# The last token pair of a fused attention and feed-forward kernel: base product undivided, maxima by halves, another order of steps

## The chip, the core and the metric

The kernel runs on one core of a Trainium2 chip. PE is the matrix engine, PEld its weight loads, DVE, ACT and POOL are the vector, scalar and general engines, and SP issues most of the transfers. The metric is the device time of one execution in microseconds; less is better.

## What is computed

The input `x` has 64 batches of 64 tokens of 1024 values, float32. Two blocks are added to it in turn:

```python
x = x + attention(conditioned(x, itok_B_0_15, W_cond))
x = x + ffn(cond2(x, itok_B_0_7))

def cond2(x, ids):                     # W: (1024, 1024), 8 experts of rank 16
    base = x @ W.T
    logits = x @ Wr.T + 5.0 * one_hot(ids)
    gates = softmax over the two largest logits, 0 elsewhere
    return base + 2.0 * einsum(x @ A.T, gates, B)

def ffn(z):                            # z rounded to bfloat16
    qg, sg = quant(z, inv_gate)        # per token: scale = max|z*inv| / 127, round, clip
    qu, su = quant(z, inv_up)
    inter = clip(silu(qg @ Wg.T * sg * s_wgate) * (qu @ Wu.T * su * s_wup), -10, 10)
    qi, si = quant(bf16(inter), inv_inter)
    return qi @ Wd.T * si * s_wdown
```

The change lies in the base product, the quantizations and what follows them, for the last 256 tokens.

## The kernel before

The attention with its output projection comes first; its result and its transpose go to device memory. From 1763.4 us on, `second_stage` works through 16 pairs (`p`), each of two tiles (`t`) of 128 tokens. Within it every instruction is issued in the order in which the helpers are called: the schedule is written by hand, three pairs deep. While pair `p` is at its base product, pair `q = p - 1` is at gate and up, and `r = p - 2` at its end. The last turn (`p, q, r` = 15, 14, 13) is a list of its own after the loop, and drains all three.

The helpers, for a pair `p` and a tile `t`:

- `router` (L1300) and `route` (DVE, small instructions L1316 to L1347) give the gates; `gates_transposed` (L1360) turns them on PE, ACT copies them to `gT`.
- `token_sums` (L1041 to L1044) makes four sums of token blocks on DVE, and `base(p, i)` (L1031) the seven products of a Strassen-Winograd scheme: the 256 x 1024 by 1024 x 1024 product is divided in 2 x 2 x 2 blocks, and seven block products of four float32 matmuls (128 x 128 by 128 x 512) take the place of eight. The weights lie in quarters `A11`, `A12`, `A22` and in combined quarters `S1` to `S4`, in tiles `wtA..` and `wtS..`. `lora` (L1365) adds the expert part by one matmul per output half. `after(p, i)` (L1389 to L1403) combines the products on DVE, two of them by an ACT copy, and writes `z` in bfloat16.
- `quant_a(p, t, nm)` for `nm` of g, u and i (gate, up, inter): multiply (L1413), maximum (L1417), scale (L1419), reciprocal (L1421) on DVE, then two roundings on ACT (L1422, L1424). `quant_b` clips on DVE (L1432) and transposes the result, by a transfer from SP (L1435), or with `by_pe=True` by matmuls (L1439) and an ACT copy (L1440).
- `gate_or_up` (L1449) is eight bfloat16 matmuls, `scaled` (L1454) multiplies by the scales on DVE and for g takes a sigmoid on ACT (L1460), `glu` (L1466 to L1469) multiplies, clips and rounds on DVE.
- `down` (L1478) is two halves of four bfloat16 matmuls; `result` multiplies by the scales (L1487) and then either hands the tile to a transfer from POOL that adds it in device memory (L1495), or adds `x` on the engine named (L1491) and stores it from SP (L1492).

Two pools of four PSUM banks, `ps_g` and `ps_h`, hold the products. A tile of a pool waits until the buffer it takes has been read by its last user. `q` and `y` in the pool `p2` have two buffers each, so have the small tiles of `sm`.

Of the kernel before, what the change touches and what calls it, by code (L numbers as in the profile page):

```python
# [11 lines left out]
F32 = mybir.dt.float32  # L12
BF16 = mybir.dt.bfloat16
# [1174 lines left out]
def second_stage(tc, a, out_t, xT_d, ident, ps_g, KC, NT, H, C, half, comb, op):  # L1188
# [12 lines left out]
    with ExitStack() as ctx:  # L1201
# [162 lines left out]
        def lora(p, ps, t, wts):  # L1364
            nc.tensor.matmul(ps, st[p]["gT"][:, t, :], wts, start=False, stop=True, skip_group_check=True)  # L1365
# [14 lines left out]

        def lora_5(p):
            lora(p, st[p]["ps", 5], 1, bm[:, hs[1]])
# [22 lines left out]
        def quant_a(p, t, nm, between=None):  # L1405
# [12 lines left out]
            sc = s["sc", nm, t] = sm.tile([P, 1], F32, tag="sc" + nm, name=f"sc_{nm}_{p}_{t}")  # L1418
# [53 lines left out]
        def down(p, t):  # L1472
            s = st[p]
            qT = s.pop(("qT", "i", t))
            for n in range(2):
                ps = s["pd", t, n] = ps_h.tile([P, HH], F32, tag="h", name=f"pd_{p}_{t}_{n}")
                for k in range(IC):
                    nc.tensor.matmul(  # L1478
                        ps, qT[:, k, :], wt_b["wd"][:, k, hs[n]], start=(k == 0), stop=(k == IC - 1)
                    )  # L1480

        def result(p, t, adds=None):
            s = st[p]
            y = p2.tile([P, H], F32, tag="y", name=f"y_{p}_{t}")
            si = s.pop(("sc", "i", t))
            for n in range(2):
                nc.vector.scalar_tensor_tensor(  # L1487
                    y[:, hs[n]], s.pop(("pd", t, n)), si, sd_w[:, hs[n]], ALU.mult, ALU.mult
                )
                if adds:  # L1490
                    adds.tensor_add(y[:, hs[n]], y[:, hs[n]], s["x", t][:, hs[n]])  # L1491
                    nc.sync.dma_start(out_t[2 * p + t, :, hs[n]], y[:, hs[n]])  # L1492
            if not adds:

                nc.gpsimd.dma_start(out_t[2 * p + t], y, accum_op=ALU.add)  # L1495

        def do(when, f, *args):
            if when:
                f(*args)
# [3 lines left out]
        for p in range(NPAIR - 1):  # L1503
# [18 lines left out]
            base(p, 7)  # L1522
            do(last, down, r, 1)
# [42 lines left out]
        token_sums(p)  # L1566
        quant_a(r, 1, "i")
        base(p, 1)
        after(p, 1)
# [3 lines left out]
        base(p, 6)  # L1573
        base(p, 7)
        gates_transposed(p)
        after(p, 6)
        quant_a(q, 0, "u")
        base(p, 2)
        after(p, 2)
        after(p, 7)  # L1580
        quant_a(q, 1, "g", (q, 0, "u"))
        down(r, 1)
        result(r, 1)
        quant_a(q, 1, "u", (q, 1, "g"))
        gate_or_up(q, 0, "g")
        scaled(q, 0, "g")
        base(p, 4)
        after(p, 4)
        gate_or_up(q, 0, "u")
        quant_a(p, 0, "g", (q, 1, "u"))  # L1590
        scaled(q, 0, "u")
        base(p, 5)
        lora_5(p)
        after(p, 5)
        quant_a(p, 0, "u", (p, 0, "g"))
        glu(q, 0)
        gate_or_up(q, 1, "g")
        quant_b(p, 0, "u")
        base(p, 3)
        scaled(q, 1, "g")  # L1600
        after(p, 3)
        gate_or_up(q, 1, "u")
        quant_a(p, 1, "g")
        gate_or_up(p, 0, "g")
        scaled(q, 1, "u")
        quant_a(p, 1, "u", (p, 1, "g"))
        gate_or_up(p, 0, "u")
        quant_a(q, 0, "i")
        glu(q, 1)
        quant_b(p, 1, "u", True)  # L1610
        gate_or_up(p, 1, "g")
        quant_a(q, 1, "i", (q, 0, "i"))
        gate_or_up(p, 1, "u")
        down(q, 0)
        scaled(p, 0, "g")
        scaled(p, 0, "u")
        quant_b(q, 1, "i")
        glu(p, 0)
        scaled(p, 1, "g")
        scaled(p, 1, "u")  # L1620
        result(q, 0)
        quant_a(p, 0, "i")
        down(q, 1)
        glu(p, 1)
        quant_b(p, 0, "i", True)
        result(q, 1, nc.gpsimd)
        quant_a(p, 1, "i")
        down(p, 0)
        result(p, 0, nc.gpsimd)
        quant_b(p, 1, "i", True)  # L1630
# [56 lines left out]
```

## Time and profile before

| | us |
|---|---|
| median of 3 runs | 2462.17 |
| lowest, highest | 2460.88, 2463.17 |
| the profiled execution, its time | 2461.01 |
| the profiled execution, its span | 2459.1 |
| start of the router of pair 15 on PE | 2376.60 |
| last base product of pair 15 starts on PE | 2412.34 |
| reciprocal of i, pair 15 tile 1, on DVE | 2445.20 |
| last down product starts on PE | 2448.87 |
| last addition on DVE starts | 2453.29 |

Times inside the execution count from the start of its span. A row of the order of instructions (the timeline) has: start, duration, engine, line, operation, output<-inputs, shapes, count, and in brackets how long the engine was idle before it and what ended that. Rows of one kind that follow each other are merged: "x8" is eight matmuls. The end of a PE row is modelled and overlaps the start of the next row by about 0.16 us. A row of busy time by stretches has: the stretch, its length, busy time of PE, PEld, DVE, ACT and POOL with the number of instructions, the clock granted to PE as a share of full speed, the share of the transfer engines, GB/s.

### The profile page before, as it was taken

The numbers are of one execution on the slowest core, as the hardware profiler recorded it, in microseconds if no ns is written. First come the engines' busy times: TensorE is split into PE (matmuls) and PEld (weight loads), VectorE is DVE, ScalarE is ACT, GpSimd is POOL, SyncE is SP. The second block draws the span as 40 slices with busy tenths as digits, with TensorE's granted clock in tenths as the row PEclk, the third lists the DMA queues.
The fourth block names the chain that finished last, engine by engine and source line by source line (L and its number), as shares of the span: only waits on it lengthen the run. The fifth ranks groups of instructions, "written<-read, shape, count | busy, mean of one in ns | idle before, by whom it ended". The sixth has DMA issues, their size and how long they took to land.

```text
span 2459.1 us, 34200 instructions
## 1 busy us (share of the span) xinstructions
PE 2423.2 (99%) x13194; PEld 1699.6 (69%) x13232; DVE 1533.1 (62%) x2957; ACT 952.8 (39%) x1303; POOL 363.4 (15%) x451
## 2 busy tenths in 40 slices
PE   8999999999999999999999999999999999999996
PEld 7888888888888888888888544444454545454452
DVE  4685585775664755745646623333367777778787
ACT  1353353342443533534424544344323333333333
POOL 5110001011122221210000233333200000000001
PEclk9999999999999999999999999999999999999998
DMA  8895767676677767775547588876744344434343
GB/s 280 284 264 152 219 200 238 188 208 210 201 198 250 206 194 246 207 208 175 177 137 234 170 258 255 263 243 215 242 126 83 84 79 88 80 81 87 70 95 72
DMA packets 417980, 446.76 MB, mean 182 GB/s; under 512 B 299665, under 2 KB 353938, under 8 KB 404114
## 3 DMA queue, kind: packets, MB, share of 16 engines
q1 hardware_dynamic: 387298, 377.90, 52.9%
q0 software_dynamic: 12080, 49.82, 7.7%
q10 hardware_dynamic: 18432, 16.79, 2.0%
q8 instruction: 106, 1.74, 0.3%
q14 instruction: 64, 0.52, 0.1%
HBM read 272.97 MB, written 100.66 MB: 152 GB/s over the span
## 4 chain that ended last, share of the span: by engine, by line
PE 94%; DVE 2%; ACT 2%; DMA 1%; issue 0%; ACTq 0%; SPq 0%; DVEq 0%
PE psva L462 5%; PE pska L435 5%; PE psvd L462 5%; PE psqa L435 5%; PE psvc L462 4%; PE pbc L1031 4%; PE pba L1031 4%; PE psqc L435 4%; PE pskc L435 4%; PE psqd L435 4%; PE pskd L435 4%; PE pbd L1031 4%; PE poa L1031 4%; PE pod L1031 4%; PE poc L1031 4%; PE s L498 3%
## 5 line engine op out<-in xcount | busy, mean ns | idle before, releaser
L540 ACT COPY pT<-phT 128x1024 int16<-128x1024 int16 x128 | 167.2, 1342 | 84.8 <-DMA phT<-ph 84.6
L514 ACT ACTIVATE prob<-prob 128x512 f32<-128x512 f32 x128 | 80.6, 630 | 259.4 <-DVE prob L511 232.1
L421 DVE SCALAR_TENSOR_TENSOR kbd<-pskd,bqkv,psku 32x256 f32<-32x256 f32 x256 | 123.1, 481 | 31.6 <-PE pskd L435 27.8
L528 ACT COPY ph<-prob 128x1024 int16<-128x1024 int16 x128 | 130.8, 1047 | 24.3 <-DVE prob L522 23.7
L1152 POOL TENSOR_TENSOR xo<-xo,ob 128x1024 f32<-128x1024 f32 x32 | 84.1, 2648 | 351.7 <-DVE To L1042 305.5
L561 ACT ACTIVATE co<-c,bqkv 128x256 f32<-128x256 f32 x128 | 60.1, 469 | 179.6 <-PE c L550 152.1
L435 PE MATMUL psqa<-yB,wq 128*128 128x256 f32 x512 | 123.6, 384 | 0.5 <-ACT psqp L406 0.5
L435 PE MATMUL pska<-yB,wk 128*128 128x256 f32 x512 | 122.6, 382 | 0.0
L1495 POOL DMA_DIRECT2D out_dram<-y x29 | 25.2, 869 | 652.3 <-DVE y L1487 652.3
L1126 ACT COPY xh<-xo 128x1024 int16<-128x1024 int16 x64 | 64.1, 1040 | 142.4 <-DVE xo L1171 142.4
L462 PE MATMUL psva<-wv,yB 128*128 128x256 f32 x512 | 117.0, 382 | 0.4
L1031 PE MATMUL poa<-woA,cx 128*128 128x512 f32 x256 | 115.4, 593 | 0.0
L1031 PE MATMUL pba<-wtA,x1T 128*128 128x512 f32 x256 | 115.1, 592 | 0.0
L1137 ACT COPY xTo<-xhT 128x1024 int16<-128x1024 int16 x64 | 84.7, 1339 | 58.4 <-DMA xhT<-xh 52.1
L435 PEld LDWEIGHTS pska<-yB,wk 128*128 128x128 f32 x512 | 96.0, 190 | 15.0 <-issue 2.6
L435 PEld LDWEIGHTS psqa<-yB,wq 128*128 128x128 f32 x512 | 95.2, 190 | 16.0 <-issue 2.8
L462 PEld LDWEIGHTS psva<-wv,yB 128*128 128x128 f32 x512 | 96.1, 190 | 14.1 <-ACT yB L363 1.0
L510 DVE TENSOR_REDUCE mx<-s 128x8 f32<-128x512 f32 x128 | 87.7, 685 | 10.7 <-PE s L498 9.3
L511 DVE TENSOR_TENSOR prob<-s,mx 128x512 f32<-128x512 f32 x128 | 88.5, 691 | 9.3 <-DVE mx L510 0.5
L522 DVE TENSOR_TENSOR prob<-prob,den 128x512 f32<-128x512 f32 x128 | 88.5, 692 | 4.4
L520 DVE TENSOR_REDUCE den<-prob 128x8 f32<-128x512 f32 x128 | 86.7, 678 | 7.2 <-ACT prob L514 6.3
L1031 PEld LDWEIGHTS poa<-woA,cx 128*128 128x128 f32 x256 | 48.4, 190 | 60.1 <-issue 59.9
(243 smaller groups left out, 5135.5 us busy)
## 6 DMA issues: line engine op xcount, KB each, us to landing
wv<-v_d SPq DMA_DIRECT2D x98, 512.0 KB, 3.9
wq<-q_d SPq DMA_DIRECT2D x28, 1792.0 KB, 7.7
wk<-k_d SPq DMA_DIRECT2D x28, 1792.0 KB, 8.1
x<-in_x_dram SPq DMA_DIRECT2D x32, 512.0 KB, 9.1
ctx_d<-co ACTq DMA_DIRECT2D x128, 128.0 KB, 4.2
cx<-ctx_d SPq DMA_DIRECT2D x16, 1024.0 KB, 6.9
xo<-in_x_dram SPq DMA_DIRECT2D x32, 512.0 KB, 5.7
xT_d<-xTo SPq DMA_DIRECT2D x64, 256.0 KB, 3.2
```

Of the source, the lines that this page charges most:

```text
L421: nc.vector.scalar_tensor_tensor(dst, ps, bias, u, ALU.add, ALU.add)
L435: nc.tensor.matmul(ps[:, 0:HB], A[:, SLOT[A_OF[i]], k, :], B[B_OF[i]][:, k, :], start=first and k == 0, stop=k == KQ - 1, skip_group_check ...
L462: nc.tensor.matmul(ps[:, j * VC:(j + 1) * VC], B[B_OF[i]][:, k, j * P:(j + 1) * P], A[:, k, :], start=first and j == 0 and k == 0, stop=k ...
L510: nc.vector.tensor_reduce(mx_v, ps, AX.X, ALU.max)
L511: nc.vector.tensor_tensor(p.rearrange("p (a e) k -> p a e k", a=2), ps, mx_v.unsqueeze(3).to_broadcast([P, 2, HPC, C]), ALU.subtract)
L520: nc.vector.tensor_reduce(den, p, AX.X, ALU.add)
L522: nc.vector.tensor_tensor(p, p, den.unsqueeze(2).to_broadcast([P, n, C]), ALU.mult)
L528: nc.scalar.copy(h, planes(p.rearrange("p n k -> p (n k)")))
L540: nc.scalar.copy(planes(pT.rearrange("p a b q -> p (a b q)")), hT)
L1031: self.nc.tensor.matmul(ps, self.B[self.B_OF[i]][:, k, :], self.A[self.A_OF[i]][:, k, :], start=first and k == 0, stop=k == self.KQ - 1, s ...
L1137: nc.scalar.copy(planes(xT.rearrange("p k q -> p (k q)")), hT)
L1152: nc.gpsimd.tensor_add(s["x"][:, t, :], s["x"][:, t, :], self.ob)
```

## The change

Four edits, all for the last pair but for one transfer in the pair before:

1. Pair 15's base product is made without the division: for each tile and each half of the columns eight float32 matmuls into one bank (`undivided`), the expert part by one more (`completed`), and a rounding copy on ACT (`rounded`). `token_sums`, `base` and `after` are not called for it. The quarter `A21`, which the divided product does not use alone, is loaded in pair 14's turn into the buffer of `S3`.
2. Tile 1 of pair 15 takes the maxima of g and u by halves of the columns (`quant_half`), joined by `quant_whole`.
3. The order of the steps of the last turn is new. The transpose of u of pair 15, tile 1, goes from PE to SP. Tile 0 of pair 15 is added half on POOL and half on DVE.
4. Buffers: `down` of pair 15 takes its banks from `ps_g`, `y` of pair 15 the buffers of `q`, and `sc` has four buffers.

```diff
+        def undivided(p, t, n):
+            s = st[p]
+            if (t, n) == (0, 0):
+                s["z"] = p2.tile([P, 2, H], BF16, tag="z", name=f"z_{p}")
+            ps = s["ps", t, n] = ps_g.tile([P, HH], F32, tag="g", name=f"pb{t}{n}_{p}")
+            for h in range(2):
+                for k in range(KQ):
+                    nc.tensor.matmul(
+                        ps, s["xT"][:, t, h * KQ + k, :], AT[f"A{n + 1}{h + 1}"][:, k, :],
+                        start=(h == 0 and k == 0), stop=(h == 1 and k == KQ - 1), skip_group_check=True,
+                    )
+        def completed(p, t, n):
+            lora(p, st[p]["ps", t, n], t, bm[:, hs[n]])
+        def rounded(p, t, n):
+            s = st[p]
+            nc.scalar.copy(s["z"][:, t, hs[n]], s.pop(("ps", t, n)))
...
+        def quant_half(p, t, nm, n):
+            s = st[p]
+            inv = ig if nm == "g" else iu
+            if n == 0:
+                s["q", nm] = p2.tile([P, H], F32, tag="q", name=f"q_{nm}_{p}_{t}")
+                s["am", nm] = sm.tile([P, 2], F32, tag="amh" + nm, name=f"amh_{nm}_{p}_{t}")
+            q = s["q", nm][:, hs[n]]
+            nc.vector.tensor_tensor(q, s["z"][:, t, hs[n]], inv[:, hs[n]], ALU.mult)
+            nc.vector.tensor_reduce(s["am", nm][:, n:n + 1], q, AX.X, ALU.max, apply_absolute_value=True)
+        def quant_whole(p, t, nm):
+            s = st[p]
+            q, am2 = s.pop(("q", nm)), s.pop(("am", nm))
+            am = sm.tile([P, 1], F32, tag="am" + nm, name=f"am_{nm}_{p}_{t}")
+            nc.vector.tensor_tensor(am, am2[:, 0:1], am2[:, 1:2], ALU.max)
+            scaled_down(p, t, nm, q, am, H)
+        def scaled_down(p, t, nm, q, am, n):
+            s = st[p]
-            sc = s["sc", nm, t] = sm.tile([P, 1], F32, tag="sc" + nm, name=f"sc_{nm}_{p}_{t}")
+            sc = s["sc", nm, t] = sm.tile([P, 1], F32, tag="sc" + nm, name=f"sc_{nm}_{p}_{t}", bufs=4)
...
-                ps = s["pd", t, n] = ps_h.tile([P, HH], F32, tag="h", name=f"pd_{p}_{t}_{n}")
+                pool, tag = (ps_g, "g") if p == NPAIR - 1 else (ps_h, "h")
+                ps = s["pd", t, n] = pool.tile([P, HH], F32, tag=tag, name=f"pd_{p}_{t}_{n}")
...
-            y = p2.tile([P, H], F32, tag="y", name=f"y_{p}_{t}")
+            y = p2.tile([P, H], F32, tag="q" if p == NPAIR - 1 else "y", name=f"y_{p}_{t}")
...
-                    adds.tensor_add(y[:, hs[n]], y[:, hs[n]], s["x", t][:, hs[n]])
+                    adds[n % len(adds)].tensor_add(y[:, hs[n]], y[:, hs[n]], s["x", t][:, hs[n]])
...
             base(p, 7)
+            if p == NPAIR - 2:
+                AT["A21"] = wa.tile([P, KQ, HH], F32, tag="wtS3", name="wtA21")
+                nc.sync.dma_start(AT["A21"], quarters(a["w_t"])[:, 0, :, 1, :])
```

The last turn from `router(p)` on, with p, q, r = 15, 14, 13, written as `step pair.tile`, the third figure of a base step a half of the columns:

```
before: router 15, down 13.0, token_sums 15, quant_a 13.1 i, base 1, after 1, route 15, quant_b 13.1 i,
 result 13.0, base 6, base 7, gates_transposed, after 6, quant_a 14.0 u, base 2, after 2, after 7,
 quant_a 14.1 g (quant_b 14.0 u), down 13.1, result 13.1, quant_a 14.1 u (quant_b 14.1 g), gate 14.0,
 scaled 14.0 g, base 4, after 4, up 14.0, quant_a 15.0 g (quant_b 14.1 u), scaled 14.0 u, base 5, lora_5,
 after 5, quant_a 15.0 u (quant_b 15.0 g), glu 14.0, gate 14.1, quant_b 15.0 u, base 3, scaled 14.1 g,
 after 3, up 14.1, quant_a 15.1 g, gate 15.0, scaled 14.1 u, quant_a 15.1 u (quant_b 15.1 g), up 15.0,
 quant_a 14.0 i, glu 14.1, quant_b 15.1 u by PE, gate 15.1, quant_a 14.1 i (quant_b 14.0 i), up 15.1,
 down 14.0, scaled 15.0 g, scaled 15.0 u, quant_b 14.1 i, glu 15.0, scaled 15.1 g, scaled 15.1 u,
 result 14.0, quant_a 15.0 i, down 14.1, glu 15.1, quant_b 15.0 i by PE, result 14.1 (POOL), quant_a 15.1 i,
 down 15.0, result 15.0 (POOL), quant_b 15.1 i by PE, down 15.1, result 15.1 (DVE)

after: router 15, down 13.0, gate 14.0, quant_a 13.1 i, undivided 15.0.0, route 15, quant_b 13.1 i,
 result 13.0, quant_a 14.0 u, down 13.1, scaled 14.0 g, gates_transposed, undivided 15.0.1,
 quant_a 14.1 g (quant_b 14.0 u), quant_a 14.1 u (quant_b 14.1 g), completed 15.0.0, 15.0.1,
 rounded 15.0.0, 15.0.1, result 13.1, quant_a 15.0 g (quant_b 14.1 u), up 14.0, undivided 15.1.0,
 completed 15.1.0, scaled 14.0 u, quant_a 15.0 u (quant_b 15.0 g), rounded 15.1.0, glu 14.0, gate 14.1,
 up 14.1, undivided 15.1.1, completed 15.1.1, scaled 14.1 g, quant_a 14.0 i (quant_b 15.0 u), scaled 14.1 u,
 glu 14.1, gate 15.0, rounded 15.1.1, quant_half 15.1 g 0, u 0, up 15.0, quant_half 15.1 g 1, quant_whole g,
 quant_b 14.0 i, quant_half 15.1 u 1, quant_whole u, down 14.0, quant_b 15.1 g, quant_a 14.1 i,
 scaled 15.0 g, scaled 15.0 u, quant_b 15.1 u, gate 15.1, glu 15.0, quant_b 14.1 i, up 15.1, quant_a 15.0 i,
 scaled 15.1 g, scaled 15.1 u, down 14.1, quant_b 15.0 i by PE, glu 15.1, quant_a 15.1 i, result 14.0,
 down 15.0, quant_b 15.1 i by PE, result 14.1 (POOL), result 15.0 (POOL, DVE), down 15.1, result 15.1 (DVE)
```

## The prediction

> **What bounds the kernel now.** I read the page first (engine sums, slices), then the busy time by stretches of the end, then the order of instructions on PE and DVE there, last the chain of waits.
>
> ```profile
> PE 2423.2 (99%) x13194; PEld 1699.6 (69%) x13232; DVE 1533.1 (62%) x2957; ACT 952.8 (39%) x1303; POOL 363.4 (15%) x451
> PE   8999999999999999999999999999999999999996
> DVE  4685585775664755745646623333367777778787
> ```
>
> PE is the bound everywhere except in the last slice. The change touches the last pair and the drain behind it, so only these matter:
>
> ```profile
> 2380.00:2400.00 20.00, 19.89 (x62) 9.18 (x63) 17.03 (x43) 7.30 (x11) 1.03 (x2) 1.00 0.41 102
> 2400.00:2420.00 20.00, 19.95 (x64) 8.84 (x62) 15.89 (x27) 7.76 (x8) 0.69 (x1) 1.00 0.45 79
> 2420.00:2440.00 20.00, 11.51 (x49) 4.97 (x48) 18.33 (x37) 9.37 (x12) 0.86 (x1) 0.83 0.19 30
> 2440.00:2460.00 20.00, 7.42 (x24) 2.46 (x24) 10.11 (x17) 3.57 (x6) 5.48 (x4) 0.59 0.35 106
> ```
>
> The columns are PE, PEld, DVE, ACT and POOL busy, then PE's clock. Until 2420 PE is full. Then DVE is (18.33 of 20), while PE starves.
>
> ```profile
> 2409.75 1.02 PE L1365 MATMUL pbd<-bm,gT 128*128 128x512 f32 x2
> 2410.61 1.89 PE L1449 MATMUL pg<-wg,qT_g 128*128 128x512 bf16 x8
> 2415.77 1.02 PE L1365 MATMUL pbd<-bmd,gT 128*128 128x512 f32 x2
> 2429.48 1.03 PE L1439 MATMUL qTp_u<-ident_b,qb_u 128*128 128x128 bf16 x8 [7.18 <-DVE qb_u L1432]
> 2430.31 3.41 PE L1449 MATMUL pg<-wg,qT_g 128*128 128x512 bf16 x8
> 2441.70 0.40 PE L1439 MATMUL qTp_i<-ident_b,qb_i 128*128 128x128 bf16 x4 [2.80 <-DVE qb_i L1432]
> 2442.78 2.81 PE L1478 MATMUL pd<-wd,qT_i 128*128 128x512 bf16 x8 [0.68 <-ACT qT_i L1440]
> ```
>
> The last base product ends at 2415.77 + 0.86 = 2416.63; the final add ends 37.35 us later:
>
> ```profile
> 2410.81 0.69 DVE L1397 TENSOR_TENSOR z<-pbd,bu 128x512 bf16<-128x512 f32 x1 [1.57 <-PE pbd L1365]
> 2437.88 0.68 DVE L1413 TENSOR_TENSOR q_i<-inter,ii 128x512 f32<-128x512 bf16 x1
> 2442.88 1.38 DVE L1413 TENSOR_TENSOR q_i<-inter,ii 128x512 f32<-128x512 bf16 x1
> 2446.81 0.71 DVE L1432 TENSOR_SCALAR qb_i<-qb_i 128x512 bf16<-128x512 bf16 x1
> 2453.29 0.69 DVE L1491 TENSOR_TENSOR y<-y,x_ll 128x512 f32<-128x512 f32 x1
> ```
>
> The same multiply takes 0.68 alone and 1.38 while POOL adds (POOL: 2442.44 to 2445.38). That price returns below.
>
> **Rules of the count, all from these rows.** A PE block occupies the distance of starts: four f32 base matmuls 3.435, a lora matmul 0.86, eight bf16 matmuls 1.73, router 3.71. DVE or ACT sees a product 0.20 after the block's slot (2410.61 to 2410.81). On DVE a dependent instruction starts 0.03 after the end, an independent one 0.08 before it. Between engines 0.03 to 0.07. A transposing DMA feeds PE 3.10 after its issue (2417.29 to 2420.40). Below, 14 and 15 are pairs, the second figure the tile, the third of z a column half.
>
> **Part 1, the undivided product.** 4 x 8 base matmuls for 7 x 4: plus 4 x 0.86 = 3.43 on PE, which is full here, so all of it is on the path. The DVE loses four token sums and five combinations at about 0.61 each (5.5 us); ACT does four rounding copies (0.57) instead of two copies. From the router's start at 2376.60: router 3.71, down 1.73, gate 1.73, product 6.87, down 1.73, gates 0.22, product 6.87, two loras 1.72, up 1.73, product 6.87, lora 0.86, gate and up 3.46, product 6.87, lora 0.86: sum 45.23, so 2421.83, **5.20 later than before**. The order of both programs shows no wait inside that is late: transposes land by 2406.7 for the matmuls at 2412.4, pd's banks are free by 2386.6 for 2390.6, and SP's new 1 MB load of A21 goes out at about 2352.2 (product 7 of pair 14 has left S3 at 2350.8), behind one transpose and ahead of the next, issued at 2361.59. Three like loads (wtA) landed after 9.3 us: 2361.5. It may slow that transpose, which has 4.3 us to spare (due at 2369.02). Price 0; if the transpose had to wait for the whole load, 9.3 - 4.3 = 5 us, a bound to which I give little weight.
>
> **Part 2, the DVE before the last half.** It waits, rather than PE: 2.8 us for z of tile 15,0 (2401.98, against 2405.52 for the same q_g before), 1.6 for pg of 14,1, 2.4 for the last half. Behind the first wait stands the clip of u of 14,1, whose transpose still lands at 2406.7 for 2412.4. So 14's and 15,0's work is done early, and tile 15,1's first-half maxima fit at 2417.7 to 2420.3. The two halves cost DVE 2 x (2 x 1.3 + 0.19) against 2 x 2.4, about 0.8 more, half of it in that idle time.
>
> **Part 3, the tail.** ACT copies the last half of z at 2422.03 to 2422.60.
> - g of 15,1: multiply 0.65, maximum 0.69, joining 0.16, scale 0.15, reciprocal 0.16, gaps: 2424.56. ACT rounds twice (1.15, 1.06): 2426.83; clip to 2427.28; DMA; PE's pg at 2430.44 to 2432.17.
> - u of 15,1: ACT is free at 2426.83, rounds to 2429.10. The clip stands behind q_i of 14,1 and two scalings on DVE: 2430.61. This transpose moves from PE to SP (about 2.1 us on PE and ACT before, 3.1 now): pu at 2433.77 to 2435.50.
> - PE waits for the transpose of i of 14,0 before its pd (2425.29 to 2427.92). Behind it stands pg of 15,1, whose own input lands at 2430.4, so price 0 at full clock.
> - DVE: ou at 2435.70, e from 2436.75 (sigmoid), then 0.67, 0.69, 0.43, 0.67, 0.69, 0.15, 0.16 and six gaps: reciprocal of i, 15,1, at 2440.39 (before: 2445.36).
> - ACT to 2441.80, DVE meanwhile y of 14,0; clip to 2442.11; PE transposes, pd at 2443.37.
> - DVE from there without a gap: y of 14,1 and 15,0 (four at 0.75), add 0.69, then twice y and add: 2448.29. Here DVE sets the end, not pd, which even at half clock (3.44) is done by 2446.8.
> - SP's and POOL's queues: SP has four transposes at 2424.8, 2427.3, 2430.7, 2433.2, each issued in 1.23, none meeting another; the last stores take 0.33 each. POOL issues y of 14,0 (0.86), then three adds instead of four, 2442.92 to 2446.73. Nothing of the end waits for its last add.
> - The buffer edits (pd of 15 in ps_g, y of 15 in q's buffers, sc four deep): the banks and buffers that they take were left by gate, up, z and the transposes of 15, all done earlier in the order. Price 0; a bank still held by a y would cost 0.75.
>
> **The port.** The two DVE adds of 2444.82 and 2446.83 read two SBUF operands while POOL's adds (1.27 each) run. Free: 0; if each waits as q_i did, 2 x 0.70 = 1.40. Walking them as in the trace (DVE waits for POOL's current add to end, POOL's next waits in turn): 2445.46 and 2447.37, together 1.08. I take that, the nearest row: end at 2449.37, against 2453.98: **minus 4.6**.
>
> **The clock.** PE now idles 2.63 (before pd of 14,0), 0.79, 1.60 and 0.76 us. The trace:
>
> ```profile
> 2425.00:2426.00 1.00, 0.00 (x0) 0.00 (x0) 0.93 (x4) 0.35 (x1) 0.00 (x0) 1.00 0.67 129
> 2427.00:2428.00 1.00, 0.00 (x0) 0.00 (x0) 0.93 (x4) 1.00 (x2) 0.00 (x0) 0.50 0.00 0
> 2444.00:2445.00 1.00, 1.00 (x4) 0.29 (x2) 0.94 (x2) 0.00 (x0) 1.00 (x1) 0.50 0.42 156
> ```
>
> The clock halves after the 7.18 us gap, and again at about 2443.6, after a gap of only 2.80, four transposes and 0.68. The Trainium skill ("TensorE: Matmul & The Clock Gate", "Why this matters for your kernels") says that only gaps above about 3 us between bursts bring the half clock back. By the rule no gap here does: price 0, gain 4.6. By the row 2.63 plus 0.79 may: then pd of 14,0 and pg take double from 2427.9 until some 3.9 us after work resumes (2429.48 to about 2433.4 in the trace); pg ends by 2433.4, before pu's input lands, price 0. Only a half clock over pu itself (2433.77) costs, 1.73. I weigh it at a tenth: 0.15. Forecast: **minus 4.5**. The profiled execution took 2461.01 (span 2459.1) and would take 2456.5; the median of runs lies 1.16 above it: 2462.17 - 4.5 = 2457.7.
>
> **The rivals.**
> - *Clock low over pu of 15,1.* For: 2.80 sufficed before. Against: PE works half the time from 2428 on. Everything from ou on slips 1.73: minus 2.8, 2459.4. Chance 0.15.
> - *No collision with POOL*, if DVE's adds fall between POOL's: minus 5.6, 2456.6. For: only adds with two SBUF operands stretched, y's did not. Against: POOL's three run back to back. Chance 0.20.
> - *Nothing gained*: every matmul block from 2427.9 on at half clock (0.50, as in the last 10 us of before): pg ends 2434.8, pu 2438.3, and pd, gap and transposes double: about minus 0.4, 2461.8. Chance 0.05.
> - *Slower*: DVE's queue, not the last product, sets the drain, so it keeps its length: 2421.83 + 37.35 = 2459.18, plus 5.2, 2467.4. The drain has to shrink by more than 5.2 us before anything is won; it decides at the first-half maxima: if DVE reaches them only after 2422.6, its backlog is intact. For: 18.33 of 20 busy. Against: from 2416.79 to the last clip's end (2447.52) DVE now idles 1.2 us, so it owes 29.5; in the count it owes 17.9 from 2422.63 to 2442.11 (19.5 less 1.6 idle), and the drain is 27.5. Chance 0.06.
>
> **The numbers.** Main case 0.54, its own range 2456.3 to 2459.1 (gain 4.5 within 0.7, and runs within 1.1). 0.2% is 4.9 us, about what a measurement of this kernel tells from no change, just beyond the main value: a good third of the main case (0.19) and most of the second rival (0.18) lie beyond it: faster 0.37. Slower 0.07, the rest 0.56. The range 2455.6 to 2460.8 takes in the main case and the first two rivals with the runs' scatter.
>
> **What would show it.** Right: PE without a gap to about 2421.8; DVE idle before hg's second half near 2422.6; reciprocal of i, 15,1, near 2440.4; the final add near 2449.4; adds of 1.2 to 1.3 on DVE beside POOL. Wrong: a PE gap before 2421, a clock of 0.50 over pu near 2434, transposes landing later than 3.1, or DVE never idle between 2398 and 2422.

## The result and the profile after

| | before | after |
|---|---|---|
| median of 13 runs each, same chip, us | 2461.25 (2458.76 to 2463.17) | 2456.86 (2455.65 to 2458.62) |
| ratio, 95% interval | | 0.9983 [0.9975, 0.9992] |
| the profiled execution (its span), us | 2461.01 (2459.1) | 2458.5 (2456.7) |
| router's start of the last turn, in the span | 2376.60 | 2377.33 |
| end of the last addition, after the router's start | 77.38 | 72.53 |
| from there to the end of the span | 5.12 | 6.84 |

The change is 4.4 us faster by the medians; the interval reaches from 2.0 to 6.2. The profiled execution of the changed kernel was the second slowest of its 13, so single times say less than the distance from the start of the last router on PE. That distance is used below for all kernels. What goes before it is the same in all of them but for the load of `A21`, which costs nothing: it landed 5.6 us after its issue at 2352.95, and the last two routers start 41.75 us apart before and 41.76 after. The rest is a shift by chance (0.73 us between these two).

The chain from the router to the last addition is 4.85 us shorter, and 1.72 us came back behind it.

The engine sums of the changed kernel's page look like those of before (DVE 1533.1 there):

```profile
PE 2423.6 (99%) x13194; PEld 1699.7 (69%) x13232; DVE 1532.9 (62%) x2955; ACT 953.2 (39%) x1304; POOL 362.9 (15%) x450
```

But the whole span hides the change. In the attention, which the change leaves alone, DVE is busy 999.59 us in this profile and 995.26 in that of before (up to 1763.4), and this chance difference covers what the last turn saves. The last turn by itself, from the router's start to the end of the span, first before, then after:

```profile
2376.60:2459.10 82.50, 62.17 (x223) 28.84 (x225) 64.46 (x126) 28.00 (x36) 8.06 (x7) 0.86 0.38 86
2377.33:2456.70 79.37, 61.11 (x223) 28.56 (x225) 59.98 (x124) 28.34 (x37) 6.76 (x6) 0.93 0.41 92
```

DVE has 4.48 us less to do there. PE has 1.06 us less although 3.43 us of products came in, since fewer matmuls of the end run at half clock (`pg` of 15,1 took 3.41 us before and takes 1.90 now) and the transposes of u of 15,1 (1.03 us) have left it.

The busy time by stretches of 20 us (the columns are PE, PEld, DVE, ACT, POOL, PE's clock, DMA share, GB/s). PE stays full to 2420 as before, and has 14.37 instead of 11.51 us in the third stretch, at a clock of 1.00 instead of 0.83. DVE has 16.07 instead of 18.33 there: its backlog is gone.

```profile
2380.00:2400.00 20.00, 19.95 (x68) 9.71 (x68) 17.07 (x44) 8.21 (x12) 0.86 (x1) 1.00 0.51 127
2400.00:2420.00 20.00, 19.95 (x59) 8.87 (x59) 14.93 (x27) 8.98 (x11) 0.86 (x1) 1.00 0.38 66
2420.00:2440.00 20.00, 14.37 (x61) 5.98 (x62) 16.07 (x36) 9.21 (x12) 0.00 (x0) 1.00 0.21 40
2440.00:2460.00 20.00, 4.17 (x17) 1.33 (x15) 9.51 (x16) 1.94 (x3) 5.04 (x4) 0.66 0.40 109
```

The order of instructions on PE from the last base product on (start, duration; in brackets the idle time ahead and what ended it; for `pg` that was the transpose of g, issued at 2428.13 and landed 3.0 us later, rather than the ACT step that the row names). Before had gaps of 7.18 and 2.80 us here; now none is over 1.97.

```profile
2421.66 1.02 PE L1365 MATMUL pb<-bm,gT 128*128 128x512 f32 x2
2428.01 1.90 PE L1521 MATMUL pd<-wd,qT_i 128*128 128x512 bf16 x8 [1.88 <-DMA qT_i<-qb_i]
2431.21 1.90 PE L1491 MATMUL pg<-wg,qT_g 128*128 128x512 bf16 x8 [1.30 <-ACT qb_i L1466]
2434.60 1.90 PE L1491 MATMUL pu<-wu,qT_u 128*128 128x512 bf16 x8 [1.49 <-DMA qT_u<-qb_u]
2443.01 0.40 PE L1481 MATMUL qTp_i<-ident_b,qb_i 128*128 128x128 bf16 x4 [1.97 <-DVE qb_i L1474]
```

On DVE, the three waits in front of the last half of `z`, the last reciprocal and the three last additions; then POOL's three additions:

```profile
2402.70 1.22 DVE L1433 TENSOR_TENSOR q_g<-z,ig 128x1024 f32<-128x1024 bf16 x1 [2.70 <-ACT z L1399]
2413.26 0.75 DVE L1496 SCALAR_TENSOR_TENSOR og<-pg,sc_g,sg_w 128x512 f32<-128x512 f32 x1 [1.47 <-PE pg L1491]
2423.33 0.69 DVE L1448 TENSOR_TENSOR q_g<-z,ig 128x512 f32<-128x512 bf16 x1 [2.33 <-ACT z L1399]
2441.04 0.16 DVE L1463 RECIPROCAL rs_i<-sc_i 128x1 f32<-128x1 f32 x1
2445.62 1.18 DVE L1534 TENSOR_TENSOR y<-y,x_ll 128x512 f32<-128x512 f32 x1
2447.49 0.98 DVE L1534 TENSOR_TENSOR y<-y,x_ll 128x512 f32<-128x512 f32 x1
2449.17 0.69 DVE L1534 TENSOR_TENSOR y<-y,x_ll 128x512 f32<-128x512 f32 x1
```

```profile
2443.75 2.50 POOL L1534 TENSOR_TENSOR y<-y,x_l 128x512 f32<-128x512 f32 x2
2446.22 1.71 POOL L1534 TENSOR_TENSOR y<-y,x_ll 128x512 f32<-128x512 f32 x1
```

DVE now waits for the last half of `z` (2.33 us) where before `z` waited for DVE. The last additions show DVE and POOL in each other's way: DVE's take 1.18 and 0.98 beside POOL's and 0.69 once POOL is done, and POOL's last one is stretched from 1.27 to 1.71.

What came back is in the last stores. The view of their line, first of the changed kernel, then of the kernel before (duration of one issue as minimum, median and maximum in ns; then microseconds from issue to landing):

```profile
L1535 SPq DMA_DIRECT2D out_dram<-y x6: 332/368/1724, 2445.0 to 2450.7; - x6
DMA to landing us min/median/max: 3.5/4.6/5.7
```

```profile
L1492 SPq DMA_DIRECT2D out_dram<-y x6: 332/332/344, 2443.7 to 2454.0; - x6
DMA to landing us min/median/max: 2.0/2.3/3.0
```

The same six stores went out in 10.3 us before and go out in 5.7 us now. The fourth issue took 1.72 us (from 2448.4 on) and held up the two behind it, so the last one begins at 2450.7, 0.8 us after its addition ended (2449.86); from there to the end of the span it is 6.0 us, against 5.1 before. These two parts make the 1.72.

### The profile page after: what moved, and what is told of

It reads as the page before. It is cut to its first block, busy times and chain, and to the rows that moved or that the text cites. A ratio compares the mean times of both kernels' runs of the same rounds, so it can differ in the third digit from the quotient of the medians.

```text
span 2456.7 us, 34195 instructions
## 1 busy us (share of the span) xinstructions
PE 2423.6 (99%) x13194; PEld 1699.7 (69%) x13232; DVE 1532.9 (62%) x2955; ACT 953.2 (39%) x1304; POOL 362.9 (15%) x450
## 4 chain that ended last, share of the span: by engine, by line
PE 95%; DVE 2%; ACT 1%; DMA 1%; issue 0%; ACTq 0%; SPq 0%; DVEq 0%
PE psva L462 5%; PE pska L435 5%; PE psvd L462 5%; PE psqa L435 5%; PE psvc L462 4%; PE psqc L435 4%; PE pskc L435 4%; PE psqd L435 4%; PE pskd L435 4%; PE pbc L1031 4%; PE pbd L1031 4%; PE pba L1031 4%; PE poa L1031 4%; PE pod L1031 4%; PE poc L1031 4%; PE s L498 3%
## 5 line engine op out<-in xcount | busy, mean ns | idle before, releaser
L1031 PE MATMUL pba<-wtA,x1T 128*128 128x512 f32 x240 | 107.9, 592 | 0.0
```

The lines of the kernel that those rows point to most:

```text
L1031: self.nc.tensor.matmul(ps, self.B[self.B_OF[i]][:, k, :], self.A[self.A_OF[i]][:, k, :], start=first and k == 0, stop=k == self.KQ - 1, s ...
```

## The experiments

All ratios are to the kernel before, run beside the kernel on the same chip. Between these sessions the median of before moves from 2460.7 to 2464.5, so times are compared by ratio, and the parts by one profile each. The intervals of most ratios overlap; what tells the kernels apart is the last addition after the router, which came at 72.53 in five profiles of kernels with the same chain. The stretch behind it is less steady: 5.9 to 6.8 in nine profiles with the same six stores.

| kernel | ratio, 95% interval | last addition after the router | stretch after it | longest issue of a last store |
|---|---|---|---|---|
| before | 1 | 77.38 | 5.12 | 0.34 |
| changed | 0.9983 [0.9975, 0.9992] | 72.53 | 6.84 | 1.72 |
| undivided, old order | 1.0010 [1.0004, 1.0017] | 79.72 | 5.09 | 0.34 |
| divided, new order | 0.9999 [0.9991, 1.0007] | 76.54 | 6.29 | 0.93 |
| same, one ACT copy later | 0.9997 [0.9989, 1.0005] | 74.98 | 6.81 | 1.06 |
| whole maxima | 0.9988 [0.9979, 0.9996] | 74.06 | 5.92 | 0.69 |
| u of 15,1 turned by PE | 0.9984 [0.9977, 0.9991] | 72.53 | 6.04 | 0.70 |
| no sum of 14,0 | 0.9982 [0.9975, 0.9988] | 72.53 | 6.02 | 0.41 |
| stores from ACT | 0.9985 [0.9978, 0.9992] | 72.53 | 5.90 | 0.42 |
| 14,0's result early | 0.9988 [0.9982, 0.9995] | 73.41 | 6.08 | 0.40 |
| halves of 15,0 exchanged | 0.9983 [0.9976, 0.9990] | 72.60 | 6.64 | 1.31 |
| 14,1 by transfer | 0.9990 [0.9983, 0.9996] | 72.56 | 6.69 | 0.66 |
| two stores only | 0.9980 [0.9973, 0.9987] | 72.53 | 5.23 | 0.34 |
| 14,1's result first | 0.9990 [0.9984, 0.9997] | 72.31 | 7.21 | 1.27 |

**The undivided product alone, in the old order.** The last turn of the kernel before, with the seven products replaced by four undivided ones at their places:

```diff
-        token_sums(p)
...
-        base(p, 1)
-        after(p, 1)
+        undivided(p, 0, 0)
...
-        base(p, 6)
-        base(p, 7)
...
-        after(p, 6)
...
-        base(p, 2)
-        after(p, 2)
-        after(p, 7)
+        undivided(p, 0, 1)
+        completed(p, 0, 0)
+        completed(p, 0, 1)
+        rounded(p, 0, 0)
+        rounded(p, 0, 1)
...
-        base(p, 4)
-        after(p, 4)
+        undivided(p, 1, 0)
+        completed(p, 1, 0)
+        rounded(p, 1, 0)
...
-        base(p, 5)
-        lora_5(p)
-        after(p, 5)
...
-        base(p, 3)
+        undivided(p, 1, 1)
+        completed(p, 1, 1)
...
-        after(p, 3)
+        rounded(p, 1, 1)
```

> Edit 1 alone: the undivided product in the old order of steps (whole maxima, old buffers, u of 15.1 by PE). Theory: PE is full up to the last base product, so 3.43 us more of matmuls put it later; walked in this order PE reaches the end of the last product about 43.5 us after the start of the router (before 40.0, after 45.2), z's last half is ready some 2.4 us later than before, and the drain behind it has its old order: 1.5 to 2.5 us slower than before. Rival (the relief of DVE by 5.5 us is what pays, whatever the order): 1 to 4 us faster than before.

Measured: slower by 0.10%, and the last addition 2.34 us later than before. DVE's waits of this kernel:

```profile
2401.66 1.61 DVE L1529 SCALAR_TENSOR_TENSOR y<-pd,sc_i,sd_w 128x512 f32<-128x512 f32 x2 [4.97 <-PE pd L1520]
2413.70 0.75 DVE L1496 SCALAR_TENSOR_TENSOR ou<-pu,sc_u,su_w 128x512 f32<-128x512 f32 x1 [3.20 <-PE pu L1491]
2423.76 1.23 DVE L1433 TENSOR_TENSOR q_g<-z,ig 128x1024 f32<-128x1024 bf16 x1 [2.94 <-ACT z L1399]
```

The end of its last base product on PE:

```profile
2422.09 1.02 PE L1365 MATMUL pb<-bm,gT 128*128 128x512 f32 x2
```

DVE has 5.5 us less to do (58.91 busy in the last turn, 64.46 before), but it spends that time waiting (11.1 us in these three), because in the old order its work comes behind PE's at each place. In the old order this edit is a loss.

**The divided product in the new order.** The changed kernel with the seven products back; the combining steps stand where the new order has its completions:

```diff
+        token_sums(p)
...
-        undivided(p, 0, 0)
+        base(p, 1)
+        after(p, 1)
+        base(p, 6)
...
+        after(p, 6)
...
-        undivided(p, 0, 1)
+        base(p, 7)
+        base(p, 2)
+        after(p, 2)
         quant_a(q, 1, "g", (q, 0, "u"))
+        after(p, 7)
         quant_a(q, 1, "u", (q, 1, "g"))
-        completed(p, 0, 0)
-        completed(p, 0, 1)
-        rounded(p, 0, 0)
-        rounded(p, 0, 1)
+        base(p, 4)
...
```

> Edit 1 undone: the divided product with its token sums and combinations on DVE, in the new order, halves and buffers kept. Theory: PE ends its last product 3.4 us earlier than with the undivided one (about 41.8 us after the router's start), but DVE, 5.5 us fuller and given tile 0 of the pair about 3.4 us later, reaches the last half of z only about 46.5 us after the router's start instead of 45.9 to 46.0: within 1 us of the changed kernel, rather slower, so about 3.5 to 4.5 us faster than before. Rival (the undivided product is what brings the gain): within 1 us of before. Rival (PE sets the end all through): about 3 us faster than the changed kernel.

Measured: no difference from the kernel before, and the last addition 4.0 us later than in the changed kernel. The expectation missed; the time is the one that its first rival named. But the trace shows an extra fault of this order:

```profile
2407.72 0.43 DVE L1474 TENSOR_SCALAR qb_g<-qb_g 128x1024 bf16<-128x1024 bf16 x1 [4.49 <-ACT qb_g L1466]
```

```profile
2404.97 0.59 ACT L1419 CAST z<-pba 128x512 bf16<-128x512 f32 x1 [4.65 <-PE pba L1365]
2405.45 1.15 ACT L1464 ACTIVATE q_g<-q_g,rs_g 128x1024 f32<-128x1024 f32 x1
```

On ACT the copy `after(p, 2)` waits 4.65 us for PE, and the rounding of `q_g` of 14,1, long ready, stands behind it. So this run doesn't tell what the division alone costs. The next one takes this wait away.

```diff
         base(p, 2)
-        after(p, 2)
         quant_a(q, 1, "g", (q, 0, "u"))
         after(p, 7)
         quant_a(q, 1, "u", (q, 1, "g"))
+        after(p, 2)
```

> The divided last product in the new order again, with one line moved: ACT's copy of z of tile 15,0 stands behind both roundings of 14,1, so that it no longer holds up q_g of 14,1. Theory (PE's 3.43 us more are covered by the DVE work that the division costs): the last product ends 3.43 us earlier than in the changed kernel, but DVE has 5.5 us more to do before the last half of z, against the 6.5 us that it idles there now: last addition 71.5 to 73.5 us after the router's start (changed kernel: 72.53), time within 1 us of the changed kernel. Rival (the undivided product itself carries the gain, even where no wait on ACT interferes): last addition at 75.5 to 77, as in the first try (76.54), some 3 us or more slower than the changed kernel.

Measured: this ACT wait is gone, 1.56 us of chain come back, and 2.45 us remain against the changed kernel. Neither expectation was right; the truth lies between them. The last base product on PE, DVE's use of it, and PE's next wait:

```profile
2423.29 1.02 PE L1365 MATMUL pbd<-bmd,gT 128*128 128x512 f32 x2
2434.05 3.60 PE L1521 MATMUL pd<-wd,qT_i 128*128 128x512 bf16 x8 [6.28 <-DMA qT_i<-qb_i]
```

```profile
2428.64 0.68 DVE L1423 TENSOR_TENSOR z<-pbd,bu 128x512 bf16<-128x512 f32 x1
```

PE has the last product at 2423.29 + 0.86 = 2424.15, but DVE takes it up only at 2428.64, without having idled since 2417: 4.5 us of backlog. PE then starves 6.28 us and works at half clock (3.60 for 1.90). The expectation had counted on filling all of the 6.5 us that DVE idles in the changed kernel; but it still idles 3.8 us on this stretch (2.19 for `pbc`, 0.5 to 0.6 three times for ACT). It also had the last product 3.43 us earlier than in the changed kernel; measured from the router it is 1.95 (43.24 against 45.19). The reason is that a fault of the kind just removed stands in this order a second time, near its start:

```profile
2391.70 0.58 ACT L1409 COPY bp<-pba 128x512 f32<-128x512 f32 x1 [2.40 <-PE pba L1031]
2392.51 0.17 DVE L1341 TENSOR_TENSOR gate<-bh,g 128x16 f32<-128x16 f32 x1 [2.21 <-ACT g L1339]
2396.41 1.90 PE L1521 MATMUL pd<-wd,qT_i 128*128 128x512 bf16 x8 [1.32 <-DMA qT_i<-qb_i]
```

ACT's copy `after(p, 1)` waits for PE, the sigmoids of the routing stand behind it, DVE waits 2.21 us for them (0.36 in the changed kernel), so the transpose of i of 13,1 is late and PE waits 1.32 us. DVE waits for PE again further on (2.19 for `pbc`), so up to 1.3 of the 2.45 us may belong to this fault and not to the division. That is an estimate from these rows; no run shows the division without it. Of the 5.5 us of DVE work that the division costs, between 1.1 and 2.45 lie on the chain.

With this run there is a table of two by two, end of the last addition after the router:

| | old order | new order |
|---|---|---|
| divided | 77.38 | 74.98 |
| undivided | 79.72 | 72.53 |

The undivided product costs 2.34 us in the old order and brings 2.45 in the new one (at least 1.1, by the estimate above). The order alone brings 2.40 (3.7 at most), and the two together 4.85. (The new order is taken with the maxima by halves and the new buffers; the buffers have no run of their own.)

**The maxima not by halves.**

```diff
         rounded(p, 1, 1)
-        quant_half(p, 1, "g", 0)
-        quant_half(p, 1, "u", 0)
...
-        quant_half(p, 1, "g", 1)
-        quant_whole(p, 1, "g")
+        quant_a(p, 1, "g")
...
-        quant_half(p, 1, "u", 1)
-        quant_whole(p, 1, "u")
+        quant_a(p, 1, "u")
```

> Edit 2 undone: tile 1 of pair 15 takes its maxima over whole rows, all else as changed. Theory: the half that lay in DVE's idle time before the last half of z now stands behind it: the clip of g 0.9 to 1.3 us and that of u 1.3 us later, the final addition 1.3 us later than in the changed kernel. Rival (the transposes or ACT set these steps): under 0.4 us.

Measured: 1.53 us later on the chain. DVE's wait in this kernel:

```profile
2425.82 1.22 DVE L1433 TENSOR_TENSOR q_g<-z,ig 128x1024 f32<-128x1024 bf16 x1 [4.97 <-ACT z L1399]
```

DVE idles 4.97 instead of 2.33 us and then has the whole width before it. This part of the change pays by using idle time, though it adds instructions.

**The u of tile 15,1 turned by PE, as before.**

```diff
-        quant_b(p, 1, "u")
+        quant_b(p, 1, "u", True)
```

> One move undone: u of tile 15.1 is transposed by PE and an ACT copy instead of a transfer from SP. Theory: pu of 15.1 ends about 0.5 us earlier, but ACT's sigmoid and DVE's clip in front of the next multiply end together with it, so the final addition moves by 0 to 0.2 us earlier. Rival (the transfer is on the path): 0.5 us or more earlier. Rival (the PE transpose, standing in front of pg of 15.1, holds it up): 0.5 us or more later.

Measured: 72.53, the same to the last digit. On this chain the transfer (3.1 us) and the way over PE and ACT are worth the same, so this move of the change brings nothing.

**The accumulating transfer of tile 14,0 left out.**

```diff
-            if not adds:
+            if not adds and (p, t) != (NPAIR - 2, 0):
```

> The changed kernel without POOL's accumulating transfer of tile 14,0 (the addition of x to that one tile is left out of the output). Theory (this transfer lies among the last stores and slows them): the last addition stays at 72.5 after the router's start, give or take 0.4, and the stretch from it to the end of the span falls from 6.84 to about 5.1 us, as in the kernel before: 1 to 1.7 us faster than the changed kernel. Rival (the six stores, now within 6 us instead of 10, get in each other's way): the stretch stays at 6 to 6.8 us, the time within 0.5 us.

```profile
L1535 SPq DMA_DIRECT2D out_dram<-y x6: 332/344/413, 2447.5 to 2452.3; - x6
DMA to landing us min/median/max: 3.3/4.1/4.4
```

Measured: the long issue is gone and the last store goes out with its addition (2452.28), but it still takes 6.0 us to the end. The rival was right: this transfer is not what lengthens the landings. The time is that of the changed kernel.

**The stores from ACT's queue.**

```diff
-                    nc.sync.dma_start(out_t[2 * p + t, :, hs[n]], y[:, hs[n]])
+                    nc.scalar.dma_start(out_t[2 * p + t, :, hs[n]], y[:, hs[n]])
```

> The changed kernel with the six last stores issued by ACT's queue instead of SP's. Theory (the transfers' engines are full there, whoever issues): one issue still takes well over 1 us, landings stay at 3.5 to 5.7 us, the stretch after the last addition at 6 to 6.8, the time within 0.5 us of the changed kernel. Rival (SP's queue itself is slow at that point): issues of 0.3 to 0.4 us and a stretch near 5.1, 1 to 1.7 us faster.

```profile
L1535 ACTq DMA_DIRECT2D out_dram<-y x6: 339/362/415, 2448.5 to 2453.3; - x6
DMA to landing us min/median/max: 3.3/3.8/4.8
```

Measured: no issue over 0.42, against both the theory and the changed kernel's own profile; but landings and stretch are as elsewhere, and the time doesn't move. The queue isn't the bound.

**Four of the six stores left out.**

```diff
+                    if (p, t) == (NPAIR - 1, 1):
-                    nc.sync.dma_start(out_t[2 * p + t, :, hs[n]], y[:, hs[n]])
+                        nc.sync.dma_start(out_t[2 * p + t, :, hs[n]], y[:, hs[n]])
```

> The changed kernel without the stores of tiles 14,1 and 15,0 (four of the six last stores left out; all additions stay). Theory (the six stores get in each other's way): the stretch after the last addition falls from about 6.0 to 5.1 or below, the landings from 3.5 to 5.7 us to 2.0 to 3.0, as in the kernel before; about 0.9 us faster. Rival (the end of the program itself is longer in the changed kernel, or the earlier accumulating transfer still lasts): the stretch stays at 5.9 or more.

```profile
L1536 SPq DMA_DIRECT2D out_dram<-y x2: 344/344/344, 2448.4 to 2449.8; - x2
DMA to landing us min/median/max: 2.0/2.8/3.5
```

Measured: the stretch falls to 5.23 and the landings to 2.0 and 3.5, with the accumulating transfer in its place. (The ratio, 0.9980, can't be told from the changed kernel's.) So the stretch is longer because six stores of 256 KB now lie within some 5 us. The busy time by stretches of the changed kernel's end shows the transfers' engines (the column before the last) full from 2444 to 2448 and nearly full for 2 us more:

```profile
2444.00:2446.00 2.00, 1.92 (x7) 0.81 (x8) 1.97 (x4) 0.03 (x1) 2.00 (x2) 0.75 0.96 113
2446.00:2448.00 2.00, 0.82 (x2) 0.00 (x0) 1.97 (x3) 0.00 (x0) 1.93 (x2) 0.50 1.01 242
2448.00:2450.00 2.00, 0.00 (x0) 0.00 (x0) 1.83 (x3) 0.00 (x0) 0.00 (x0) 0.50 0.84 305
```

With two stores these shares are 1.02, 0.76 and 0.35. The first 2 us are the accumulating transfer in both; what differs is the stores.

**The halves of tile 15,0 exchanged.**

```diff
-        result(p, 0, nc.gpsimd, nc.vector)
+        result(p, 0, nc.vector, nc.gpsimd)
```

> The changed kernel with the halves of tile 15,0's last addition exchanged: DVE adds the first half, POOL the second. Theory (SP's queue holds a ready store back: in the changed kernel the store of the half that DVE has finished at 2446.8 stands behind that of the half that POOL finishes at 2447.9, so three to four stores go out together): the first half's store goes out about 1.2 us earlier, the last addition stays at 72.5 after the router's start within 0.3, and the stretch after it falls from about 6.0 (5.9 to 6.3 in five of the runs; 6.84 in the changed kernel's own profile) to 5.2 to 5.6; 0.4 to 0.8 us faster. Rival (the bytes of six stores in 5 us are what counts, not their order): 5.9 to 6.2, no difference.

```profile
2445.14 1.54 DVE L1534 TENSOR_TENSOR y<-y,x_ll 128x512 f32<-128x512 f32 x1
```

Measured: the first addition no longer waits (0.69), the second now waits longer (1.54), the chain is the same (72.60) and the stretch 6.64. It is no shorter, so the order of these stores does not help, as the rival had it, though 6.64 lies above the rival's 5.9 to 6.2 too; one issue took 1.31 us in this profile.

**Three tries for a better end.** The result of 14,0 moved ahead of the products of 15,0:

```diff
         gate_or_up(p, 1, "g")
+        result(q, 0)
         glu(p, 0)
...
         quant_a(p, 1, "i")
-        result(q, 0)
```

> The changed kernel with the result of tile 14,0 (two scalings on DVE, then POOL's accumulating transfer) moved ahead of the products of tile 15,0, so that the transfer starts about 10 us earlier. Theory: the transfer lands before the first of the last stores; the stretch after the last addition falls to about 5.1 to 5.5 us. On DVE the 1.4 us now stand where it idles 0.33 and 0.37 us, so the reciprocal of i of 15,1 comes about 0.7 us later, and the wait for its rounding is filled with the result of 14,1 instead: last addition 0 to 0.7 us earlier than 72.53. Together 1.3 to 2.2 us faster than the changed kernel. Rival (the end of the chain is PE's, at half clock, so that what comes later on DVE comes later at the end; and the stores collide anyway): last addition at 73.2 or later, no gain.

```profile
2443.53 1.90 PE L1521 MATMUL pd<-wd,qT_i 128*128 128x512 bf16 x8 [2.60 <-DMA qT_i<-qb_i]
```

Measured: 0.88 us later on the chain and a stretch of 6.08. The two scalings also stand ahead of the clip of i of 14,1, so its transpose and `pd` come later (PE waits 2.60), and the wait for the last rounding is not filled with 14,1's result, which is issued behind the clip: DVE idles 1.45 us there. The transfer issued 10 us earlier changed nothing at the end.

Then tile 14,1 by a second accumulating transfer, and both halves of 15,0 added by POOL:

```diff
-        result(q, 1, nc.gpsimd)
-        result(p, 0, nc.gpsimd, nc.vector)
+        result(q, 1)
+        result(p, 0, nc.gpsimd)
```

> The changed kernel with x added to tile 14,1 by a second accumulating transfer of POOL's, as for 14,0, and both halves of tile 15,0 added by POOL: DVE has one addition of 0.69 (1.18 with its wait) less, and POOL two additions less in front of 15,0. Theory (DVE's queue sets the last addition): 1.1 to 1.6 us earlier on that chain, 70.9 to 71.4 after the router's start; the stores fall from six to four. Rival (the accumulating transfers fill the transfers' engines: one of 512 KB took a share of 16.4% of 21 us, 3.4 us of all sixteen, against 20.4% for three times the bytes of plain stores): with two of them and four stores, about 9.7 us of transfers between 2443.7 and the end, the stretch after the last addition grows to 7 us or more and takes the gain back.

```profile
2444.80 2.22 DVE L1534 TENSOR_TENSOR y<-y,x_ll 128x512 f32<-128x512 f32 x1
2447.72 0.69 DVE L1534 TENSOR_TENSOR y<-y,x_ll 128x512 f32<-128x512 f32 x1
```

Measured: one addition less on DVE, and yet 72.56: the first of the two waited for both of POOL's additions, back to back (2.22). The four stores landed after 4.5 to 5.8 us, and the stretch is 6.69. Slower than the changed kernel by about 0.07% by the ratios, within their intervals.

Last, 14,1's result first and 14,0's in front of DVE's addition to 15,0:

```diff
-        def result(p, t, *adds):
+        def result(p, t, *adds, between=None):
...
+                if between and n == 1:
+                    between()
...
-        result(q, 0)
+        result(q, 1, nc.gpsimd)
...
-        result(q, 1, nc.gpsimd)
-        result(p, 0, nc.gpsimd, nc.vector)
+        result(p, 0, nc.gpsimd, nc.vector, between=lambda: result(q, 0))
```

> The changed kernel with the result of tile 14,1 (and POOL's two additions to it) in the place of that of 14,0, and the result of 14,0 with its accumulating transfer between the scalings of 15,0 and DVE's addition to its second half. POOL's three additions then start about 1.7 us earlier and end at about 68.3 after the router's start, before DVE adds for the first time (68.9). Theory (DVE's 0.49 and 0.29 of waiting behind POOL's additions are on the chain that sets the end): all three DVE additions take 0.69, the last one ends 0.7 to 0.8 us earlier, 71.7 to 71.9 after the router's start, and since the stores are a little further apart the stretch after it is not longer: 0.7 us or more faster than the changed kernel, ratio to the kernel before 0.9976 to 0.9981. Rival (the accumulating transfer of 14,0, now issued about 2.9 us later, lies among the last stores): the chain is shorter all the same, but the stretch after the last addition grows to 7.3 us or more, and the time is that of the changed kernel or worse.

```profile
2443.60 0.77 DVE L1474 TENSOR_SCALAR qb_i<-qb_i 128x512 bf16<-128x512 bf16 x1
2446.93 0.67 DVE L1536 TENSOR_TENSOR y<-y,x_ll 128x512 f32<-128x512 f32 x1
```

```profile
L1537 SPq DMA_DIRECT2D out_dram<-y x6: 332/404/1271, 2444.2 to 2450.6; - x6
DMA to landing us min/median/max: 2.0/4.1/6.1
```

Measured: all additions of DVE take 0.67 to 0.69, as expected, but the clip of i of 15,1 now falls beside POOL's additions and takes 0.77 instead of 0.29, so the chain gains only 0.22. The accumulating transfer, now issued at 2447.3 among the last stores, lengthens the stretch to 7.21, just under the 7.3 that the rival named. The rival decided it. None of these versions beats the changed kernel.

## Why the prediction was right

**The chain.** Forecast 4.6 us shorter, measured 4.85. With the router 0.73 later in this profile, its marks come at:

| mark | forecast, moved by 0.73 | measured |
|---|---|---|
| end of the last base product | 2422.56 | 2422.52 |
| `pd` of 14,0 on PE | 2428.65 | 2428.01 |
| `pg` of 15,1 | 2431.17 | 2431.21 |
| `pu` of 15,1 | 2434.50 | 2434.60 |
| end of the reciprocal of i, 15,1 | 2441.12 | 2441.20 |
| `pd` of 15,1 | 2444.10 | 2444.08 |
| end of the last addition | 2450.10 | 2449.86 |

*Part 1* (PE 3.43 us more, nothing inside late, the load of A21 hidden) holds: the load had landed before the next transpose went out at 2362.32; the first mark fits to 0.04 us, and PE has 19.95 of 20 us in both stretches ahead of it. *Part 2* (DVE waits instead of PE) holds in each of its three waits: 2.8, 1.6 and 2.4 forecast, 2.70, 1.47 and 2.33 measured. The run without halves confirms the use of that idle time. *Part 3* holds but for one size: the transpose of i of 14,0 (128x512) landed 2.4 us after its issue, not the 3.10 counted from a larger one; as argued, nothing hung on it, since `pg` behind it waited for its own input.

**DVE's additions beside POOL's.** Their waiting was taken as 1.08 us and measured 0.49 + 0.29 = 0.78; that accounts for the 0.25 us by which the chain came out shorter than counted. The rival without a collision is out. That DVE's waiting is real shows in the run with 14,1's result first, where the same additions, clear of POOL's, take 0.69.

**The clock.** Granted at 1.00 until 2445.0 over gaps of 1.88, 1.30, 1.49 and 1.97 us, then 0.50, when only `pd` of 15,1 was left. So the rival with half clock over `pu` is out: `pu` took 1.90 us. Up to there the profile agrees with the Trainium skill ("TensorE: Matmul & The Clock Gate", "Why this matters for your kernels"), whose table warns of gaps above about 3 us between bursts; that shorter ones never bring the half clock back is the prediction's reading of it. At the end it does not: the half clock came after gaps of 1.97 and 0.68. Nor does the row of before (2.80 and 0.68) give a rule, for in the runs with 1.92 to 1.99 and 0.68 us of idle time ahead of the last `pd`, it took anything from 1.90 to 3.52 us. Here it is in the run with two stores and in the one with u turned by PE:

```profile
2444.00 1.90 PE L1521 MATMUL pd<-wd,qT_i 128*128 128x512 bf16 x8 [0.68 <-ACT qT_i L1482]
2445.98 3.29 PE L1521 MATMUL pd<-wd,qT_i 128*128 128x512 bf16 x8 [0.68 <-ACT qT_i L1482]
```

The last addition ends at 72.53 in both. So DVE sets the end even with `pd` at half clock, as Part 3 had it: price 0.

**What it missed** is the time behind the last addition. The forecast carries the difference at the final add ("2449.37, against 2453.98") whole to the end of the span, and so takes the 5.12 us behind it as unchanged. It measured 6.84 in this profile, and 5.9 to 6.8 in eight other profiles with the same six stores behind one another. The text had looked at SP's queue (0.33 for each issue) but not at what six stores of 256 KB do when their distance is halved: a shorter DVE tail starts its transfers closer together, and they collide. By the profiles the sum is then between -4.85 + 0.8 and -4.85 + 1.72, so 3.1 to 4.1 us gained; the medians say 4.4 (4.5 was forecast) with an interval of 2.0 to 6.2, which holds all of these. The forecast of the gain is thus closer than its sum deserves: the chain gave 0.25 more than counted, and the stores took about 1 back. That it fits the medians to 0.1 us is in part luck.

**The rival that ends slower** has its mechanism confirmed by one run, though not its case. In the undivided product with the old order the last product ends 43.46 us after the router's start (2422.09 + 0.86 - 2379.49), 3.43 later than before (40.03), and the drain behind it falls only from 37.35 to 36.26 us, so the end comes 2.34 later. In the changed kernel the product comes 5.16 later, but the drain is 27.34 us. In the divided product with the new order (one ACT copy later) DVE's backlog of 4.5 us keeps the drain at 31.74.

**Open.** Why one issue of a store took 1.72 us in the changed kernel's profile and 0.70 with the same stores in the run with u turned by PE is not settled; there is one profile of each. Not settled either are when the half clock comes after gaps of about 2 us, and what the divided product would give in an order in which no ACT copy holds up a step that is ready.

## What to carry to other kernels

Relieving the second engine was worth nothing here until the order let it use the time: on the chain the same edit was a loss of 2.3 us in one order and a gain of 1.1 to 2.5 in the other, so an edit and its order must be costed together, by asking at each step which of the two engines waits. When a tail gets shorter, count again what it sends out in that time: transfers that were hidden by their distance begin to collide. And in an engine's queue look for the instruction that waits ahead of one that is ready: a single copy on ACT cost 1.56 us of chain. And read engine sums for the stage that was changed: over the whole span the 4.5 us that DVE saved did not show.

## What the runs showed of the hardware

- Six stores of 256 KB within 5 to 6 us landed after 3.1 to 5.7 us, against 2.0 to 3.0 when they were spread over 10 us, and 2.0 and 3.5 when only two of them went out. Beyond the scatter (a stretch of 5.9 to 6.8 us) it made no difference whether SP or ACT issued them, in which order, or whether the accumulating transfer ahead of them was left out. Issued among them (one profile), that transfer did cost: the stretch after the last addition rose to 7.21 us.
- A store's issue on SP, 0.33 us as a rule, took up to 1.72 us in the changed kernel's profile, in which the transfers' engines had shares of 0.84 to 1.01. In the profile with the stores on ACT, with shares up to 1.01 too, none took over 0.42.
- DVE instructions of two SBUF operands waited for POOL's additions: 1.18 and 0.98 behind one of them, 2.22 behind two in a row, against 0.69 alone. A bf16 clip of one operand did so too (0.77 for 0.29), while scalings with an operand in PSUM kept their 0.74.
- The half clock came or did not come after the same two gaps of PE (1.92 to 1.99 and 0.68 us): the last `pd` took from 1.90 to 3.52 us.
- A transposing transfer of 128x512 bf16 landed 2.4 us after its issue, one of 128x1024 after 3.0 to 3.1.
